# Bilinear operands written once and read with a repeating step, and matmul operands widened to 128 rows

## The chip, the cores and the metric

The kernel runs on one core of one Trainium2 chip. The metric is device time in microseconds of that core, from launch to end. A profile shows one execution of the same program: the busy times of the engines, the packets of the DMA queues, and what ended each engine's idle times. Engines are named as in the profile: PE is TensorE's matmul, PEld its load of the stationary operand, DVE is VectorE, ACT is ScalarE, POOL is GpSimd, SP is SyncE, which here only issues DMAs.

## The reference

The input is an image batch of shape (16, 56, 56, 128) in fp32. Four layers follow one another, each as `x = x + layer(group_norm(x))`:

- layer 0 is attention within shifted windows of 7 x 7 with 4 heads;
- layer 1 is a triangle update: a layer norm over the 128 channels, gated projections, a product over one image axis, a second layer norm, an output projection and a gate;
- layer 2 is a Fourier operator with an attention over the 56 rows and two spectral convolutions;
- layer 3 is the bilinear layer, which the change mostly concerns. Cut to what matters:

```python
xp = silu(x @ W1) @ W2
q, k, v = xp[..., :128], xp[..., 128:144], xp[..., 144:]   # each l2-normed; q is 8 heads of 16
K_H1 = conv2d(k, H1_w, groups=16) + P1                     # 3 x 7, per position a 16 x 16 matrix
kernel = einsum('xnk,xkd->xnd', q, K_H1)                   # per position x
feature = conv2d(v, H2_w)                                  # 16 x 16 per position
V_G = conv2d(v, G_w) + I                                   # 16 x 16 per position
feature = einsum('xvw,xvd->xwd', V_G, feature)
out = einsum('xnd,xvd->xvn', kernel, feature)
```

So each of the 3,136 positions of an image has three small products of an operand `y` with a matrix that a convolution of 21 taps (3 x 7) has made for that position.

## The kernel before, in words

An image lies in SBUF with the 128 channels on the partitions and its 3,136 positions along the free dimension, and is worked on in 7 chunks of 448 positions (`CH`, `NCH`). Images go through the four layers in turn. Each image belongs to one of two lanes (`lane[0] = b % 2`). A lane has its own arena of SBUF, its own five `w2` tiles of [128, 512], two PSUM banks `psb`, one PSUM tile `psd` of two banks, and twelve DRAM tiles `dy`. So two images are under way at a time. The order of the instructions on each engine isn't written out by hand: a planner runs through the program with its own estimates of the durations, gives out the tiles' buffers, and writes each engine's instructions in the order in which they came up there. On the chip each engine and each issuing queue (SP's, ACT's, POOL's) then keeps that order. The only orders given by hand are those of `together`, which lets the other matmuls of a group follow its first.

**The bilinear layer** (`_bilinear`). In the loop over `q`, chunk `q + 2` is projected (`project`), chunk `q - 2` goes through the feature product, chunk `q` through the kernel product, and chunk `q - 4` is finished (`last`).

`project` makes the 128 query rows of a chunk and hands them to `kept` (L1314 on): ACT copies them from PSUM to a `w2` tile `t` (L1317) and issues a DMA from ACT's queue (L1318) which writes the tile to DRAM eight times over: each row of `dy` is [8, 448], eight copies of one row of `t`. `project` also makes the 32 rows of k and v. PE turns them (L1361) to partitions 96 to 127 of a PSUM bank, ACT copies them (L1363) into one of two `staged` pieces of the arena, which sit in partitions 96 to 127 of its first 992 columns and have zeros at the borders, and three DMAs of ACT's queue (L1368) write them to the padded planes in DRAM.

`spread` (L1377) reads those planes back with four DMAs of SP's queue, so that each of 84 partitions of `im` holds one channel of k or v shifted by one of the 21 taps; row 84 holds ones and carries `P1` or `I`. The ones come from a memset of partitions 64 to 95 of the arena (L1304). `conv` multiplies these 85 rows by the weights `l3wk`, `l3wf` or `l3wg`: for `l3wf` two matmuls of 85 x 128 per half (L1391), otherwise groups of four of 85 x 32 through `together` (L368 the first, L371 the rest). ACT copies the result to `zs` (L1398).

`contract` forms one product. Four times it reads two of the four parts of `y` from DRAM into a buffer `rep` of [128, 2, 448] (L1410, SP's queue, four buffers), in which partition `a * 8 + k` holds row `a` of a part, for k from 0 to 7; DVE multiplies it by both halves of `z` (L1413, 128 x 1,792 elements, three buffers `prods`), and groups of eight matmuls by `red` (L368, L371) add up over the partitions into `acc`. The result of the first two products goes to DRAM through `kept` again.

**The layer norms** (`layer_norm` in `_triangle`, two per image). A matmul by `cen` takes off the mean; squares are averaged by matmuls that leave chunk `q` in row `32 * (q % 4) + q // 4` of one PSUM bank; ACT and DVE make 1/sqrt of it in `rs` (all 128 rows hold finite numbers). Then per chunk a matmul (L651) copies that one row of `rs` to all 128 partitions: its stationary operand is a column of the identity, stepped by 0 to 128 columns, of the 32 rows that hold it, and its moving operand the same 32 rows of `rs`. DVE multiplies (L652) and ACT scales (L653).

Of the kernel before, what the change touches and what calls it, by code (L numbers as in the profile page):

```python
# [36 lines left out]
F32 = mybir.dt.float32  # L37
# [5 lines left out]
P = 128  # L43
T = 56
# [3 lines left out]
CH = 448  # L48
# [156 lines left out]
def _weights(i):  # L205

    g = {k: np.asarray(v) for k, v in i.items()}
    w, early = {}, {}
# [20 lines left out]
    for n, key in (("a", "L2_conv_wQ"), ("b", "L2_conv_wK")):  # L229
        k = g[key][:, 0]  # L230
# [46 lines left out]

    wk3, wg3 = (np.zeros((85, 4, 2, 4, 8), np.float32) for _ in range(2))  # L280
    wf3 = np.zeros((85, 4, 16, 8), np.float32)
    for u in range(16):
        rows = slice(u % 4 * 21, u % 4 * 21 + 21)
        wk3[rows, u // 4, :, u % 4] = h1[u].reshape(2, 8, 21).transpose(2, 0, 1)
# [2 lines left out]
    wk3[84] = g["L3_conv_P1"][0].reshape(4, 4, 2, 8).transpose(0, 2, 1, 3)  # L287
    wg3[84] = g["L3_conv_I"][0].reshape(4, 4, 2, 8).transpose(0, 2, 1, 3)
    for n, v in (("l3wk", wk3), ("l3wf", wf3), ("l3wg", wg3)):
        w[n] = v.reshape(85, -1)  # L290
    return w, early, late


# [14 lines left out]
def tile_blocks(ctx: ExitStack, tc: tile.TileContext, ins, out, at, stages=(0, 1, 2, 3)):  # L308
# [22 lines left out]
    def uid(s):  # L331
        count[0] += 1
        return f"{s}{count[0]}"
# [14 lines left out]
        return ps2[lane[0]].tile([P, 2, 512], F32, tag="ps2", name=uid("psd"))  # L348

    def dram():  # L350
        return dyp[lane[0]].tile([P, 8 * CH], F32, tag="dy", name=uid("dy"))

    def bc(ap, axis, n):

# [260 lines left out]
def _triangle(env):  # L615
# [5 lines left out]
    def layer_norm(chunk, dst, sqs, lw, lb):  # L621


        for q in range(NCH):
            d, sq = dst[:, q * CH : (q + 1) * CH], sqs[:, q * CH : (q + 1) * CH]
            src = chunk(q)
            p = e.psb()
            mm(p[:, :CH], lhsT=C("cen"), rhs=src, start=True, stop=True)
            act(sq, p[:, :CH], AF.Square)
            nc.vector.tensor_copy(d, p[:, :CH])  # L630

        pv = e.psb()
        e.together(
            dict(
                out=pv[32 * (q % 4) : 32 * (q % 4) + 32, :CH],
                lhsT=C("oh")[:, 1 - q // 4 : 33 - q // 4],
                rhs=sqs[:, q * CH : (q + 1) * CH],
                start=q < 4,
                stop=q > 2,
            )  # L640
            for q in range(NCH)
        )
        rs = e.w2()
        act(rs[:, :CH], pv[:, :CH], AF.Sqrt, bias=eps)
        nc.vector.reciprocal(rs[:, :CH], rs[:, :CH])
        for q in range(NCH):
            d = dst[:, q * CH : (q + 1) * CH]
            s = slice(32 * (q % 4), 32 * (q % 4) + 32)
            p = e.psb()
            row = 32 * (q % 4) + q // 4  # L650
            mm(p[:, :CH], lhsT=C("ident")[s, row : row + 1].to_broadcast([32, P]), rhs=rs[s, :CH], start=True, stop=True)  # L651
            tt(d, d, p[:, :CH], ALU.mult)  # L652
            act(d, d, AF.Identity, bias=W("ln")[:, lb : lb + 1], scale=W("ln")[:, lw : lw + 1])  # L653

# [622 lines left out]
def _bilinear(env):  # L1277
# [20 lines left out]
    def run(b, xt):  # L1298
# [2 lines left out]
        kv_dram = padded[e.lane[0]]  # L1301

        im = [ar[:, 4 * SPAN * k : 4 * SPAN * (k + 1)] for k in range(2)]
        nc.gpsimd.memset(ar[64:96, 0 : 8 * SPAN], 1.0)  # L1304

        staged = [ar[96:P, k * SPAN : (k + 1) * SPAN] for k in range(2)]
        nc.gpsimd.memset(ar[96:P, 0 : 2 * SPAN], 0.0)
        zs = [ar[:, 3968 + k * 896 : 4864 + k * 896] for k in range(4)]
        reps = [ar[:, 7552 + k * 896 : 8448 + k * 896] for k in range(4)]
        prods = [ar[:, 11136 + k * 1792 : 12928 + k * 1792] for k in range(3)]  # L1310
# [3 lines left out]
        def kept(p):  # L1314

            t, d = e.w2(), e.dram()
            nc.scalar.copy(t[:, :CH], p[:, :CH])  # L1317
            nc.scalar.dma_start(out=d.rearrange("p (k t) -> p k t", k=8), in_=bc(t[:, :CH], 1, 8))  # L1318
            return d

        def project(q):
# [37 lines left out]
            p = e.psb()  # L1359
            for a in range(4):  # L1360
                mm(p[96:P, a * TT : (a + 1) * TT], lhsT=kv[:, a * 32 : (a + 1) * 32], rhs=C("ident")[:TT, :TT], start=True, stop=True)  # L1361
            t = staged[q % 2]
            nc.scalar.copy(  # L1363
                t.rearrange("p (r j) -> p r j", j=PITCH)[:, :, 3 : 3 + T],
                p[96:P, :CH].rearrange("p (r j) -> p r j", j=T),
# [16 lines left out]
        def conv(w, i, slot):  # L1382

            z = zs[slot]
            rows = im[i][:85].rearrange("p (g r j) -> p g r j", g=4, j=PITCH)[:, :, :, :T]
            wt = W(w)
            p = e.psd()
            for h in range(2):
                if w == "l3wf":
                    for g in (2 * h, 2 * h + 1):  # L1390
                        mm(p[:, h, :CH], lhsT=wt[:, g * P : (g + 1) * P], rhs=rows[:, g], start=g == 2 * h, stop=g == 2 * h + 1)  # L1391
                else:
                    e.together(
                        dict(out=p[32 * g : 32 * g + 32, h, :CH], lhsT=wt[:, (2 * g + h) * 32 : (2 * g + h + 1) * 32], rhs=rows[:, g], start=True, stop=True)
                        for g in range(4)
                    )
            z = z.rearrange("p (h t) -> p h t", h=2)
            nc.scalar.copy(z, p[:, :, :CH])  # L1398
            return z

        def contract(y, z):

            acc = e.psb()
            yv = y.rearrange("(i n a) (k t) -> n (a k) i t", n=2, a=D, k=8)
            for n in range(2):
                done = []
                for two in (0, 2):
                    rep = reps[count[1] % 4].rearrange("p (i t) -> p i t", i=2)
                    count[1] += 1
                    nc.sync.dma_start(out=rep, in_=yv[n][:, two : two + 2, :])  # L1410
                    t4 = prods[count[2] % 3].rearrange("p (i h t) -> p i h t", i=2, h=2)
                    count[2] += 1
                    tt(t4, bc(rep, 2, 2), bc(z, 1, 2), ALU.mult)  # L1413
                    done += [t4[:, 0], t4[:, 1]]
# [83 lines left out]
```

## Time and profile before

| what | value |
|---|---|
| median of 3 runs | 13,561.23 us (13,510.66 to 13,577.86) |
| the profiled execution | 13,592.43 us; span 13,590.7 us |
| PE busy | 10,774.2 us (79%), 82,624 matmuls |
| DVE busy | 9,629.1 us (71%) |
| ACT busy | 3,845.5 us (28%) |
| POOL busy | 1,391.0 us (10%) |
| mean granted TensorE clock | 0.832 |
| DMA | 1,091,753 packets, 2,105.90 MB |
| of it dy written (ACT's queue, q10) | 336 DMAs of 1,792 KB |
| of it dy read (SP's queue, q1) | 1,344 DMAs of 448 KB |
| of it padded planes read (q1) | 896 DMAs of 162.8 KB |
| of it Fourier table (POOL's queue, q0) | 2,048 DMAs of 294 KB |

The page cuts the span into 40 equal slices of 340 us; each digit is a tenth of busy time in a slice, or of the full clock. A pair of images takes some 1,700 us, five slices. A line of a group gives the line of the code, engine, operation, result and operands with their shapes, how often, then the busy time, the mean duration in ns, and the engine's idle time just before with what ended it. q1 is SP's DMA queue, q10 ACT's, q0 POOL's; a line of a queue gives packets, MB and the share of the time of all 16 DMA engines.

### The profile page before, as it was taken

The page shows a single profiled execution, that of the slowest core. Times are in us where ns is not written, and L with a number is a line of the kernel's source. Part 1 is how long each engine was busy: PE and PEld are TensorE (multiplying, and loading weights), DVE is VectorE, ACT ScalarE, POOL GpSimd, SP SyncE. Part 2 cuts the span into 40 slices and gives each one's busy share as a digit, 9 for nine tenths or more (in the row PEclk, how much of TensorE's full clock was granted, in tenths as well). Part 3 has the DMA queues.
Part 4 walks back from the last instruction along what each step waited for, and adds up shares of the span by engine and source line. Part 5 has one row for each costly group of instructions (what it writes and reads, how often), then busy time and mean ns, then how long its engine had stood idle before and what let it go on. Part 6 is the DMA issues. An engine that isn't in the chain of part 4 may idle for free. (4 is left out here: it accounts for less than half of the span.)

```text
span 13590.7 us, 201886 instructions
## 1 busy us (share of the span) xinstructions
PE 10774.2 (79%) x82624; PEld 5938.7 (44%) x82624; DVE 9629.1 (71%) x13985; ACT 3845.5 (28%) x6630; POOL 1391.0 (10%) x2650
## 2 busy tenths in 40 slices
PE   7888787886878878887788877887777887778876
PEld 4454254542545335443354433544335543355432
DVE  7776868757686685776767768667686676866766
ACT  4232141321423223232242322322224222242221
POOL 0120002200022000220002200022000220002200
PEclk9887888878988887887888888878788888888877
DMA  1246804378044770447704577044680446804468
GB/s 34 85 149 243 294 1 125 115 252 278 5 130 111 265 261 5 118 132 250 267 7 117 143 270 237 7 117 128 222 293 13 117 128 230 288 10 117 132 230 276
DMA packets 1091753, 2105.90 MB, mean 155 GB/s; under 512 B 98320, under 2 KB 974096, under 8 KB 1089680
## 3 DMA queue, kind: packets, MB, share of 16 engines
q1 hardware_dynamic: 560000, 823.95, 18.5%
q0 software_dynamic: 165120, 629.61, 17.1%
q10 hardware_dynamic: 365712, 639.44, 13.0%
q8 instruction: 654, 10.72, 0.3%
q14 instruction: 267, 2.19, 0.1%
HBM read 1412.73 MB, written 667.03 MB: 153 GB/s over the span
## 5 line engine op out<-in xcount | busy, mean ns | idle before, releaser
L1413 DVE TENSOR_TENSOR arena<-arena 128x1792 f32<-128x1792 f32 x1344 | 2656.5, 2018 | 713.8 <-PE psb L371 314.6
L1203 DVE TENSOR_TENSOR arena<-arena 112x1344 f32<-112x1344 f32 x1024 | 1571.3, 1553 | 383.1 <-DMA arena<-table 372.6
L371 PE MATMUL psb<-arena,cst 128*32 128x448 f32 x9792 | 1600.8, 682 | 0.0
L368 PE MATMUL psb<-arena,cst 128*32 128x448 f32 x1408 | 836.6, 683 | 766.2 <-DVE arena L1413 675.2
L1201 POOL DMA_DIRECT2D arena<-table x2048 | 1064.8, 521 | 2647.2 <-PE psb L1117 610.6
L371 PE MATMUL psb<-arena 112*64 112x224 f32 (+2 forms) x4864 | 1252.8, 528 | 0.0
L368 PE MATMUL psb<-arena 112*64 112x448 f32 (+1 forms) x1280 | 697.5, 630 | 368.7 <-DVE arena L1094 178.5
L371 PE MATMUL psd<-arena 112*64 112x224 f32 (+1 forms) x3072 | 746.7, 464 | 0.0
L368 PE MATMUL psd<-arena 112*64 112x448 f32 x1024 | 552.4, 625 | 214.3 <-DVE arena L1203 200.9
L371 PEld LDWEIGHTS psb<-arena 112*64 112x64 f32 (+1 forms) x4864 | 440.9, 153 | 512.8 <-issue 509.7
L1094 DVE TENSOR_TENSOR arena<-w,coef 128x1792 f32<-128x1792 f32 x256 | 507.6, 2020 | 190.9 <-PE psb L371 167.4
L679 PE MATMUL psd<-wgt,arena 128*64 128x128 f32 x7168 | 549.8, 303 | 102.9 <-DVE arena L691 79.4
L368 PEld LDWEIGHTS psb<-arena,cst 128*32 128x32 f32 x1408 | 123.3, 122 | 1137.4 <-DVE arena L1413 818.2
L1398 ACT COPY arena<-psd 128x896 f32<-128x896 f32 x336 | 303.5, 906 | 1022.2 <-DVE arena L1413 581.4
L371 PEld LDWEIGHTS psb<-arena,cst 128*32 128x32 f32 x9792 | 373.6, 127 | 485.9 <-issue 468.5
L679 PEld LDWEIGHTS psd<-wgt,arena 128*64 128x64 f32 x7168 | 472.0, 151 | 246.1 <-issue 163.8
L371 PE MATMUL psd<-arena,wgt 85*32 85x448 f32 x2688 | 528.6, 624 | 40.7 <-DMA arena<-padded 40.1
L908 PE MATMUL psb<-cst,arena 128*128 128x64 f32 (+1 forms) x2688 | 452.9, 341 | 55.5 <-ACT arena L918 30.6
L908 PEld LDWEIGHTS psb<-cst,arena 128*128 128x128 f32 x2688 | 438.7, 255 | 104.6 <-issue 51.7
L368 PE MATMUL psd<-arena,wgt 85*32 85x448 f32 x896 | 449.8, 619 | 41.6 <-DMA arena<-padded 34.1
L1317 ACT COPY w<-psb 128x448 f32<-128x448 f32 x336 | 178.7, 532 | 1032.5 <-PE psb L371 728.8
L589 PE MATMUL psb<-cst,arena 128*49 128x128 f32 x2048 | 345.5, 326 | 146.1 <-DVE arena L584 87.7
(299 smaller groups left out, 19630.8 us busy)
## 6 DMA issues: line engine op xcount, KB each, us to landing
arena<-table POOLq DMA_DIRECT2D x2048, 294.0 KB, 9.1
dy<-w ACTq DMA_DIRECT2D x336, 1792.0 KB
arena<-dy SPq DMA_DIRECT2D x1344, 448.0 KB
arena<-padded SPq DMA_DIRECT2D x896, 162.8 KB
w<-x SPq DMA_DIRECT2D x112, 224.0 KB
out<-w SPq DMA_DIRECT2D x112, 224.0 KB
padded<-arena ACTq DMA_DIRECT2D x336, 62.0 KB
arena<-arena POOLq DMA_DIRECT2D x16, 784.0 KB, 9.9
```

The lines of the kernel that those rows point to most:

```text
L368: done = mm(**first)
L371: mm(**kw)
L589: nc.tensor.transpose(p[:WIN, i * P : (i + 1) * P], s3[:, 4 * g + i, :], C("ident"))
L679: mm(p[half : half + 64, i // 4, i % 4 * P : (i % 4 + 1) * P], lhsT=xh[:, c0 : c0 + 64], rhs=W(w).rearrange("p (k c) -> p k c", c=64)[:, : ...
L908: mm(p[:, 2 * i * nl : 2 * (i + 1) * nl], lhsT=src[:, t * P : (t + 1) * P], rhs=fc, start=True, stop=True)
L1094: tt(t4, bc(ys[c][:, l0 : l0 + 4, :], 1, 8), bc(coef[:, c, h0 : h0 + 8, l0 : l0 + 4], 3, T), ALU.mult,)
L1201: nc.gpsimd.dma_start(out=t[hh * T : (hh + 1) * T, :], in_=bc(tflat[q, two, hh], 0, T))
L1203: tt(t4, bc(x3[:, :, s], 1, 2), t4, ALU.mult)
L1317: nc.scalar.copy(t[:, :CH], p[:, :CH])
L1398: nc.scalar.copy(z, p[:, :, :CH])
L1413: tt(t4, bc(rep, 2, 2), bc(z, 1, 2), ALU.mult)
```

## The change

Four edits, in the words of the code:

- `dy` becomes [128, 448] instead of [128, 3,584]. `kept` writes each row once. Row p of `t` is i * 32 + r, with i the part (0 to 3); it now goes to place (r, i), so that the four parts of one row lie side by side. `contract` reads two parts at once as 896 elements in a row, and names each row eight times by a step of 0 in the source.
- The weights `l3wk`, `l3wf`, `l3wg` get 128 rows, of which rows 85 to 127 are zero, and `conv` multiplies all 128 rows of `im`. So the memset of ones covers partitions 64 to 127, and rows 85 to 127 hold ones against weights of zero.
- With partitions 96 to 127 of the arena taken by these ones, the staging tile of k and v becomes a `w2` tile of each chunk, zeroed by a memset on POOL before ACT's copy.
- The norms' spread takes all 128 rows of the identity's column and of `rs` in place of 32.

```diff
-    wk3, wg3 = (np.zeros((85, 4, 2, 4, 8), np.float32) for _ in range(2))
-    wf3 = np.zeros((85, 4, 16, 8), np.float32)
+    wk3, wg3 = (np.zeros((P, 4, 2, 4, 8), np.float32) for _ in range(2))
+    wf3 = np.zeros((P, 4, 16, 8), np.float32)
...
-        w[n] = v.reshape(85, -1)
+        w[n] = v.reshape(P, -1)
...
-        return dyp[lane[0]].tile([P, 8 * CH], F32, tag="dy", name=uid("dy"))
+        return dyp[lane[0]].tile([P, CH], F32, tag="dy", name=uid("dy"))
...
-            s = slice(32 * (q % 4), 32 * (q % 4) + 32)
             p = e.psb()
             row = 32 * (q % 4) + q // 4
-            mm(p[:, :CH], lhsT=C("ident")[s, row : row + 1].to_broadcast([32, P]), rhs=rs[s, :CH], start=True, stop=True)
+            mm(p[:, :CH], lhsT=C("ident")[:, row : row + 1].to_broadcast([P, P]), rhs=rs[:, :CH], start=True, stop=True)
...
-        nc.gpsimd.memset(ar[64:96, 0 : 8 * SPAN], 1.0)
-
-        staged = [ar[96:P, k * SPAN : (k + 1) * SPAN] for k in range(2)]
-        nc.gpsimd.memset(ar[96:P, 0 : 2 * SPAN], 0.0)
+        nc.gpsimd.memset(ar[64:P, 0 : 8 * SPAN], 1.0)
...
-            nc.scalar.dma_start(out=d.rearrange("p (k t) -> p k t", k=8), in_=bc(t[:, :CH], 1, 8))
+            nc.scalar.dma_start(out=planes(d, 0, ((CH, 4), (4 * CH, 32), (1, CH))), in_=t[:, :CH])
...
-            t = staged[q % 2]
+
+            t = e.w2()[96:P, :SPAN]
+            nc.gpsimd.memset(t, 0.0)
...
-            rows = im[i][:85].rearrange("p (g r j) -> p g r j", g=4, j=PITCH)[:, :, :, :T]
+            rows = im[i].rearrange("p (g r j) -> p g r j", g=4, j=PITCH)[:, :, :, :T]
...
-            yv = y.rearrange("(i n a) (k t) -> n (a k) i t", n=2, a=D, k=8)
...
-                    rep = reps[count[1] % 4].rearrange("p (i t) -> p i t", i=2)
+                    rep = reps[count[1] % 4]
                     count[1] += 1
-                    nc.sync.dma_start(out=rep, in_=yv[n][:, two : two + 2, :])
+                    nc.sync.dma_start(out=rep, in_=planes(y, (n * D * 4 + two) * CH, ((4 * CH, D), (0, 8), (1, 2 * CH))))
+                    rep = rep.rearrange("p (i t) -> p i t", i=2)
```

## The prediction

> **What bounds the kernel now.** I read the page's slices first, then its queues, then the bilinear stage of one pair of images in stretches of 100 us, then the waits, and last the chain of the final pair. The slices (DVE, granted clock, DMA share) repeat every five: the two last of each five are the bilinear stage.
>
> ```profile
> DVE  7776868757686685776767768667686676866766
> PEclk9887888878988887887888888878788888888877
> DMA  1246804378044770447704577044680446804468
> q1 hardware_dynamic: 560000, 823.95, 18.5%
> q0 software_dynamic: 165120, 629.61, 17.1%
> q10 hardware_dynamic: 365712, 639.44, 13.0%
> ```
>
> No engine is full on average, but DMA stands at 7 to 8 tenths in the bilinear slices, and inside them (columns: window, PE, PEld, DVE, ACT, POOL busy, clock, DMA share, GB/s) it fills up:
>
> ```profile
> 4500.00:4600.00 100.00, 79.83 (x378) 39.52 (x378) 58.30 (x110) 20.50 (x37) 4.32 (x2) 0.77 0.78 271
> 4700.00:4800.00 100.00, 81.07 (x496) 33.15 (x492) 67.22 (x63) 16.63 (x26) 0.00 (x0) 0.83 0.95 325
> 4800.00:4900.00 100.00, 68.92 (x472) 24.89 (x464) 84.18 (x62) 15.42 (x25) 0.00 (x0) 0.85 1.00 357
> ```
>
> DVE does 58 to 84 us of 100, PE 69 to 81, DMA 78 to 100: three near-limits, of which DMA is the only one that reaches its end. Who waits for it, over the whole span (busy, mean ns, idle before):
>
> ```profile
> L1413 DVE TENSOR_TENSOR arena<-arena 128x1792 f32<-128x1792 f32 x1344 | 2656.5, 2018 | 713.8 <-PE psb L371 314.6 <-DMA arena<-dy 264.5 <-ACT arena L1398 110.0
> L371 PE MATMUL psd<-arena,wgt 85*32 85x448 f32 x2688 | 528.6, 624 | 40.7 <-DMA arena<-padded 40.1
> L368 PE MATMUL psd<-arena,wgt 85*32 85x448 f32 x896 | 449.8, 619 | 41.6 <-DMA arena<-padded 34.1 <-ACT arena L1398 7.4
> L651 PE MATMUL psb<-w,cst 32*128 32x448 f32 x448 | 219.2, 804 | 76.2 <-DVE w L645 51.1 <-DVE arena L652 18.3 <-DVE sm L1053 4.4
> L990 PE MATMUL psb<-arena,cst 128*128 128x448 f32 x672 | 367.6, 672 | 39.2 <-DVE arena L987 13.7 <-ACT arena L985 12.2 <-ACT arena L1022 6.9
> ```
>
> The page's chain sums to a fifth of the span only, the last stretch, so I read it for the last two pairs' bilinear windows of 720 us. In the last, `DMA arena<-dy` holds 10.8%, `DMA dy<-w` 8.7% and `DMA arena<-padded` 4.2%: 78, 63 and 30 us; in the pair before 76, 24 and 24. Average: 77 + 44 + 27 = 148 us a pair. Single writes of dy held it for 7 to 18 us.
>
> **The Trainium skill.** (1) TensorE: Matmul & The Clock Gate, Part 1 (The HAM clock gate): an activity monitor gives the array half or full clock, by windows of 3,413 ns. The trace agrees: its clock record knows only 0.5 and 1.0, in steps of 3.413 us, 34% of them at half, and a 448-column matmul took 539 ns at full and 954 at half. (2) The same page, Part 3 (Packing small matmuls): [...]several run at once. It agrees: 301 of L651's 448 matmuls overlap the next (219.2 us covered, 448 x 804 ns = 360 in sum). (3) DMA: Bandwidth & Descriptors, Why a DMA increments its semaphore by 16: a transfer uses the largest k up to 16 that divides both sides' slowest dimension. It agrees: q10's 365,712 packets are 336 x (1,024 + 16) for dy, 336 x (32 + 16) for the planes, 144 for the weights, so one packet of semaphore for each of 16 engines.
>
> **The change part by part.**
>
> Writes of dy. Now 336 x 1,024 = 344,064 packets at q10's mean (13.0% x 16 x 13,590.7 us / 365,712) = 77 ns: 1,656 us of all 16 engines, 207 a pair. After: 128 packets each, 207 us in all. The new destination's slowest dimension is 4, so by (3) only four engines carry it: 32 packets, 2.5 us, where 64 on each of 16 took 4.9. Those four get 103 us a pair, less than the 207 before. DMA saved: 1,449 us, 181 a pair.
>
> Reads of dy. Bytes stay (616.6 MB), packets go from 256 of 1,792 B to 128 of 3,584 B; 16 engines still (16 divides 128). Whether eight reads of one place cost more, no dy row shows; the nearest is the Fourier table, whose rows are read 56 times. q1 takes 2,514 us for 824 MB, 3.05 us/MB; the table 3.69. So 1,881 us before, between 10% less (fewer packets) and 2,276 (+395) after. I take +100; DMA net -1,350.
>
> What that moves: the chain. A write falls from 12.5 us (the mean of seven) to about 5 (2.5 plus the 1.7 us in which the small padded writes land on the same chain, and some queueing), 44 to 18 us a pair; reads, queued less, from 7.0 to 4.5, 77 to 50; padded from 27 to 20. That is 60 us a pair, 480 in all, if nothing else takes over. It will: PE is 69 to 81% busy there, and L1413 also waits 314.6 us for PE and 110 for ACT. The direct waits (264.5 + 40.1 + 34.1 = 339 us) are the other measure; 60% of them is 203. I take 300.
>
> Staging through w2. One 0.92 us memset per image goes; the 3.40 us one covers 64 rows for 32 at the same length; seven memsets of [32, 496] come, 0.46 us each (half of 992 columns at 920 ns). They lie between the squares (L1345) and the copy (L1363), 1.6 to 20 us, median 8.7 apart, so 0 on the path. Without that cover: 112 x 0.46 = 52 us. If one is late, L1363 is, and behind it on ACT the padded writes and the other image's copies; DVE and PE wait for those. A staged tile holds one of five w2 slots until its writes land; a dy tile holds its own for fewer us. Even.
>
> Issue. L1318 blocks ACT's queue 0.52 us, L1410 SP's 0.365; three-dimensional L1377 takes 0.76. At worst +0.25 x 336 = 84 us on ACT (28% busy) and +0.4 x 1,344 = 538 on SP, 34 an image of some 550: no cost, unless padded reads (on SP behind them) get late, +20.
>
> Convolutions at 128 rows. Same columns, same time at a clock. What can move is the gate. I summed per 3.413 us step, over the matmul records, active rows x columns / 16,384 x 1.25 ns a moving column. This ranks a warm next step above a cold one in 98% of cases from warm (94% from cold); with rows ignored 97% (87%). The state flips near 0.43 to 0.50 of the array. With 128 rows in both edits, the same curve leaves 384 us fewer at half clock (143 from the convolutions, 241 from the norms) of 4,540. Each such us of matmuls shrinks to 0.56; PE holds 9 of the chain's 21 parts: 384 x 0.44 x 0.43 = -70. If rows don't count: 0.
>
> Norms' spread. 448 matmuls that overlapped take turns now: at the present half-and-half clock 448 x 745 ns = 334 us for 219, warm 260. On its own image it stays under ACT's L653 (755 ns); the other image's PE work is delayed by a third of 40 to 115 us: +20 (0 to 115).
>
> Sum: -300 - 70 + 20 = -350. Against the profiled execution's span of 13,590.7 (1.7 us lie around it): 13,241. The runs' median is 0.23% below that execution: 13,210.
>
> **Rivals.** *Hidden* (0.15): the planner's order and PE set the stage; PE is near 80% busy at a clock of 0.77 where DVE has only 58, and the saved DMA waits return as waits for PE. Gain 30 to 100: about 13,500. *POOL's queue* (0.15), slower: POOL's order is written by the planner, and a staging memset may stand behind the other image's arena memset or L536, which wait up to 107.7 us (L1304 for PE) and 56 us (81 waits, 1,328.6 us). From 26 us per image (418/16) the change ends slower by 0.5%; 35 us give 13,770. Against it: POOL is otherwise idle there, and memsets are planned by readiness. A reordered plan in general goes here. *Repeated reads* (0.10), slower: above 310 ns per 3,584 B packet ((207 + 235 - 26) us x 16 / 21,504) DMA is as full as before; the table's rate means 211, today's 175. Then about 13,750. *The forecast* (0.60): 12,950 to 13,450.
>
> **How the numbers follow.** Within 0.5% is what a measurement can't tell from no change (13,493 to 13,629). Faster: 0.60 + 0.06 of hidden = 0.66; same: 0.09 of hidden and 0.01; slower 0.24. The range runs from 12,950 to 13,700, leaving out some 0.05 below and 0.12 above; the forecast's own is 12,950 to 13,450.
>
> **What would show it.** q10 at about 60,600 packets (336 x (128 + 4) for dy if four engines carry it) and 100 MB; q1 at 388,000; total near 1,566 MB; DMA slices at 4 to 6; L1413's wait for dy under 100 us; clock from 0.832 to about 0.86; L651 at 128 rows, 540 to 700 ns; L1363 with no wait for POOL. Wrong if L1413's idle time keeps its 714 us under other names, if ACT waits for POOL, or if the packets of the reads pass 210 ns.

## The result, and the profile after

| | before | after |
|---|---|---|
| median, 14 runs each | 13,577.55 us (13,510.66 to 13,612.31) | 13,655.42 us (13,602.10 to 13,721.09) |
| profiled span | 13,590.7 us | 13,715.4 us |
| mean granted TensorE clock | 0.832 | 0.835 |

The changed kernel takes 1.0059 times as long (95% interval 1.0039 to 1.0079): some 80 us slower, where 350 us less were forecast. The profiled execution of after is one of its longer ones; the two spans differ by 125 us, the medians by 78.

The page of the changed kernel, its slices and queues:

```profile
DVE  7866867777666776767767676676766767767675
PEclk9987888888887888977888788897788878888877
DMA  1354704455045550455504455045550445504545
q1 hardware_dynamic: 387968, 823.95, 21.1%
q0 software_dynamic: 165120, 629.61, 17.2%
q10 hardware_dynamic: 60624, 99.93, 2.6%
```

The transfers did what the change says. ACT's queue (q10) writes 100 MB where it wrote 639, and the bilinear slices stand at 4 to 5 tenths of DMA (after the first pair) where they stood at 6 to 8. The same three stretches of a pair's bilinear stage (columns: window, PE, PEld, DVE, ACT, POOL busy, clock, DMA share, GB/s):

```profile
4500.00:4600.00 100.00, 80.31 (x695) 46.08 (x693) 60.13 (x99) 29.36 (x54) 2.00 (x5) 0.82 0.49 139
4700.00:4800.00 100.00, 72.41 (x436) 30.15 (x429) 68.24 (x77) 16.90 (x30) 1.52 (x3) 0.83 0.66 195
4800.00:4900.00 100.00, 72.76 (x428) 37.59 (x427) 59.80 (x105) 24.15 (x41) 4.83 (x11) 0.76 0.43 119
```

DMA has room now, 0.43 to 0.66, and yet PE and DVE aren't busier than before: averaged over the three stretches PE does 75 us of 100 where it did 77, DVE 63 where it did 70 (the lanes stand differently, so a stretch doesn't hold quite the same work in both). The groups that wait (busy, mean ns, idle before, and what ended it):

```profile
L1411 DVE TENSOR_TENSOR arena<-arena 128x1792 f32<-128x1792 f32 x1344 | 2665.3, 2019 | 942.9 <-PE psb L371 400.8 <-DMA arena<-dy 299.6 <-ACT arena L1396 212.2
L371 PE MATMUL psd<-arena,wgt 128*32 128x448 f32 x2688 | 508.1, 615 | 39.7 <-DMA arena<-padded 39.4
L368 PE MATMUL psd<-arena,wgt 128*32 128x448 f32 x896 | 448.1, 617 | 92.4 <-DMA arena<-padded 89.9 <-ACT arena L1396 2.3
L650 PE MATMUL psb<-w,cst 128*128 128x448 f32 x448 | 208.7, 577 | 34.9 <-DVE w L645 32.0 <-DVE arena L651 2.9
L989 PE MATMUL psb<-arena,cst 128*128 128x448 f32 x672 | 356.0, 659 | 78.5 <-ACT arena L984 33.2 <-ACT arena L1021 22.1 <-DVE arena L1245 11.3
```

The products of the bilinear stage (L1413 before, L1411 now) wait 943 us where they waited 714: for dy 300 us instead of 265, although dy's transfers are lighter, for PE 401 instead of 315, for ACT 212 instead of 110. PE's waits for padded keys (L371 and L368 with `psd`) went from 74 us to 129. No single new wait has taken the place of an old one; most of the old ones have grown.

One more view tells what kind of thing has changed. Each image's bilinear stage begins with POOL's memset of ones, so its start times mark where the two lanes stand. Its line for the last pair, images 14 and 15, before (durations in ns, then first and last start in us):

```profile
L1304 POOL MEMSET arena<- x2: 3398/3398/3398, 12839.4 to 13128.1; 32x3968 f32 x2
```

and after:

```profile
L1303 POOL MEMSET arena<- x2: 3404/3404/3404, 12876.5 to 13303.4; 64x3968 f32 x2
```

The odd lane stands 289 us behind the even one before, 427 us after. Nothing in the four edits moves a lane against the other. The order of the instructions does: the planner, given other instructions, has written another one.

### The profile page after: what moved, and what is told of

Same layout as the page of the kernel before. It is cut to its first block, busy times and chain, and to the rows that moved or that the text cites. A ratio compares the mean times of both kernels' runs of the same rounds, so it can differ in the third digit from the quotient of the medians.

```text
span 13715.4 us, 202688 instructions
## 1 busy us (share of the span) xinstructions
PE 10697.2 (78%) x82624; PEld 5921.2 (43%) x82624; DVE 9630.0 (70%) x13985; ACT 3916.2 (29%) x6686; POOL 1460.0 (11%) x2746
## 3 DMA queue, kind: packets, MB, share of 16 engines
q10 hardware_dynamic: 60624, 99.93, 2.6%
## 5 line engine op out<-in xcount | busy, mean ns | idle before, releaser
L1411 DVE TENSOR_TENSOR arena<-arena 128x1792 f32<-128x1792 f32 x1344 | 2665.3, 2019 | 942.9 <-PE psb L371 400.8
L371 PE MATMUL psb<-arena,cst 128*32 128x448 f32 x9792 | 1626.3, 688 | 0.0
L368 PE MATMUL psb<-arena,cst 128*32 128x448 f32 x1408 | 840.5, 686 | 828.2 <-DVE arena L1411 723.1
L371 PE MATMUL psb<-arena 112*64 112x224 f32 (+2 forms) x4864 | 1291.3, 537 | 0.0
L368 PE MATMUL psb<-arena 112*64 112x448 f32 (+1 forms) x1280 | 721.9, 651 | 425.4 <-DVE arena L1093 214.5
L371 PE MATMUL psd<-arena 112*64 112x224 f32 (+1 forms) x3072 | 773.1, 476 | 0.0
L368 PE MATMUL psd<-arena 112*64 112x448 f32 x1024 | 568.4, 641 | 204.0 <-DVE arena L1202 192.6
L371 PEld LDWEIGHTS psb<-arena 112*64 112x64 f32 (+1 forms) x4864 | 448.3, 156 | 526.3 <-issue 520.6
L368 PEld LDWEIGHTS psb<-arena,cst 128*32 128x32 f32 x1408 | 119.9, 121 | 1180.1 <-DVE arena L1411 891.0
L678 PE MATMUL psd<-wgt,arena 128*64 128x128 f32 x7168 | 509.4, 290 | 107.4 <-DVE arena L690 100.6
L371 PEld LDWEIGHTS psb<-arena,cst 128*32 128x32 f32 x9792 | 377.1, 127 | 486.7 <-issue 469.2
L371 PE MATMUL psd<-arena,wgt 128*32 128x448 f32 x2688 | 508.1, 615 | 39.7 <-DMA arena<-padded 39.4
L368 PE MATMUL psd<-arena,wgt 128*32 128x448 f32 x896 | 448.1, 617 | 92.4 <-DMA arena<-padded 89.9
```

The source lines that it names most:

```text
L368: done = mm(**first)
L371: mm(**kw)
L678: mm(p[half : half + 64, i // 4, i % 4 * P : (i % 4 + 1) * P], lhsT=xh[:, c0 : c0 + 64], rhs=W(w).rearrange("p (k c) -> p k c", c=64)[:, : ...
```

## The experiments

All ratios are to the kernel before, run on the same chip in the same batch; its median lies between 13,560 and 13,578 us in every batch, so ratios of different batches can be compared. Where spans or waits are compared, they are those of one profiled execution of each kernel; that of after is 60 us above its median. The diffs are abridged: `NoSync` and `only` stand for longer expressions. All kernels do the whole work of the reference. Those of the experiments have a few lines more than the two kernels, so L1432 or L1444 in their profiles are the products (L1413 before), and L374 and L371 the members and the first of `together`.

### The edits, or the order they were put in

The planner's order was taken apart from the edits. A kernel is planned, each engine's order is kept as a list of instruction numbers, and another kernel with the same instructions in number is planned with that list as a constraint. The constraint adds an edge from each instruction to the next on its engine, without any semaphore:

```diff
+    for e, ks in order.items():
+        for a, b in zip(ks, ks[1:]):
+            tc.add_manual_dep(mine[e][b], mine[e][a].name, NoSync, reason="order")
```

Only the staging memsets, which one kernel has in other numbers than the other, are left to the planner. The traces show that the order was taken over: compared place by place by operation, tiles and shape, VectorE's 13,985 instructions and SP's 2,506 in e1 come in the sequence of the kernel before, and those of e2 in that of the changed kernel; the changed kernel itself has only 2,330 of VectorE's at the place where the kernel before has them. e1 is the changed kernel in the order of the kernel before, e2 the kernel before in the order of the changed one. e3 has the bilinear operands alone (the edits of `dram`, `kept` and `contract`), e4 the convolutions alone (the weights, `conv`, the memsets, the staging), each in the order that the planner makes for it.

> All four edits, but every engine and queue keeps the order that the planner wrote for the kernel before (order-only edges; only the 112 new staging memsets on POOL are placed freely). Theory plan (the edits are a gain of about 50 us of each image's bilinear layer, and the changed kernel lost it because the planner wrote another order): ratio to before 0.97 to 0.985, about 13,250 us. Theory edits (the repeated reads at 199 ns a packet and the staging cost what the writes gain, the order is beside the point): 1.000 to 1.010, about 13,650 us.

> The kernel before, instruction for instruction, in the order that the planner wrote for the changed kernel. Theory plan: slower than both, ratio 1.015 to 1.04, 13,800 to 14,100 us, since the worse order is there and the saved transfers are not. Theory edits: 0.995 to 1.005.

> Only the first edit: dy written once, read with the repeating step; convolutions at 85 rows, staging in the arena, the norms' spread at 32 rows; the planner's own order for it. Theory plan: this edit changes the planner's estimates most, so the order moves as in the changed kernel: 1.000 to 1.010. Theory edits, reads to blame: 1.003 to 1.010 as well; staging to blame: 0.97 to 0.985.

> Only the convolutions at 128 rows and with them the staging tile in w2; dy written eight times, the norms' spread at 32 rows; the planner's own order. Theory plan: within 0.99 to 1.01, as the order falls. Theory edits, staging to blame: 1.010 to 1.03, with ACT's copy of the staged rows waiting. If the clock follows the declared rows, mean clock above 0.838.

| work, order | ratio (95% interval) |
|---|---|
| e1: changed, before's order | 0.9823 (0.9786 to 0.9861) |
| e2: before's, changed order | 1.0222 (1.0189 to 1.0256) |
| e3: bilinear operands, own order | 1.0198 (1.0164 to 1.0233) |
| e4: convolutions, own order | 1.0004 (0.9984 to 1.0024) |

e3 was slower than either theory had it. e4 lies where "plan" had it, but its granted clock (median 0.8315) did not pass the 0.838 that was expected if the clock follows the rows. The answers of e1 and e2 are clear. In the old order the edits gain 1.8% (240 us of 13,571). With no edit at all, the new order costs 2.2%. Their product is 1.004; the changed kernel has 1.006. The groups of e1:

```profile
L1432 DVE TENSOR_TENSOR arena<-arena 128x1792 f32<-128x1792 f32 x1344 | 2654.8, 2019 | 557.5 <-PE psb L374 303.9 <-DMA arena<-dy 147.9 <-ACT arena L1412 87.3
L374 PE MATMUL psd<-arena,wgt 128*32 128x448 f32 x2688 | 486.1, 591 | 22.9 <-DMA arena<-padded 22.3
L371 PE MATMUL psd<-arena,wgt 128*32 128x448 f32 x896 | 426.5, 592 | 42.2 <-DMA arena<-padded 34.1 <-ACT arena L1412 8.1
```

With the same instructions as the changed kernel, the products wait 558 us, not 943, and for dy 148, not 300. In e2 the instructions are those of the kernel before, and the wait for dy grows from 265 to 416:

```profile
L1432 DVE TENSOR_TENSOR arena<-arena 128x1792 f32<-128x1792 f32 x1344 | 2670.5, 2021 | 1057.7 <-DMA arena<-dy 416.0 <-PE psb L374 403.8 <-ACT arena L1412 212.9
```

So e1 is faster than both kernels, by edits that are the change's own.

### What each edit gains in the old order

Three kernels with one group of edits each, in the order of the kernel before.

> The bilinear operands written once with repeating reads alone, without the convolutions and norms, in the order of the kernel before. It splits the 1.8% that the whole change gains in that order. 'The gain is the transfers' (shorter write, a read that doesn't wait): 0.980 to 0.988, nearly all of it, with VectorE's waits for dy down by some 100 us. 'The gain is the clock' (convolutions at 128 rows keep TensorE's clock up): 0.997 to 1.002 here, and the rest in the run of the convolutions.

> The convolutions over 128 rows (with the weights' zero rows, the ones below them and the staging in a work tile) alone, without the bilinear operands and norms, in the order of the kernel before. 'The gain is the clock': 0.984 to 0.990, granted clock 0.845 or more. 'The gain is the transfers': 0.996 to 1.002, granted clock 0.83 to 0.84. My estimate on record for the clock part was 70 us, 0.995.

> The layer norms' spread over 128 rows alone, in the order of the kernel before. The whole change gains 1.77% there; the bilinear operands alone gained 0.79% and the convolutions 0.45%, which leaves 0.5%. 'The parts add up': 0.993 to 0.997, with a higher clock. My estimate on record was a loss of 20 us (0 to 115): 1.0015, at most 1.0085. 'The parts help each other' (the rest comes only when dy and the clock go together): 0.998 to 1.002.

| edit alone, before's order | ratio (95% interval) | us | median clock of its runs |
|---|---|---|---|
| none | 1 | | 0.831 |
| e7: bilinear operands | 0.9921 (0.9891 to 0.9951) | -107 | 0.835 |
| e8: convolutions, with the staging | 0.9955 (0.9937 to 0.9973) | -61 | 0.838 |
| e11: norms' spread | 0.9961 (0.9942 to 0.9981) | -53 | 0.839 |
| sum | 0.984 | -221 | |
| e1: all | 0.9823 (0.9786 to 0.9861) | -240 | 0.851 |

The parts add up, as e11's first expectation had it. Neither pure theory of e7 and e8 holds: about half of the gain comes with the transfers and half with the wider matmuls. In e7 the wait for dy falls by 131 us (265 to 133.5):

```profile
L1444 DVE TENSOR_TENSOR arena<-arena 128x1792 f32<-128x1792 f32 x1344 | 2653.7, 2018 | 589.9 <-PE psb L374 328.5 <-DMA arena<-dy 133.5 <-ACT arena L1424 111.0
```

In e8 the products' idle time hardly changes (714 to 683 us), and the matmuls of the convolutions get shorter, 624 to 609 ns. In the records of before and e8 a matmul of 448 columns takes 538 or 539 ns at full clock and 954 at half (medians), with 85 rows as with 128, so what has changed is how much of it runs at full clock:

```profile
L374 PE MATMUL psd<-arena,wgt 128*32 128x448 f32 x2688 | 509.7, 609 | 28.1 <-DMA arena<-padded 27.9
```

In e11 the estimate on record, a loss of 20 us, was a miss. The spread at 128 rows is busy 235 us, only 16 more than the 219 at 32 rows, and each matmul takes 640 ns where it took 804:

```profile
L663 PE MATMUL psb<-w,cst 128*128 128x448 f32 x448 | 235.2, 640 | 70.7 <-DVE w L657 52.0 <-DVE arena L664 11.9 <-DVE sm L1065 4.4
```

Since e3 and e7, and e4 and e8, are the same work in two orders, the order that the planner makes for the bilinear operands alone costs 2.8% (1.0198 / 0.9921), and the one for the convolutions 0.5%.

### The distance of the lanes

The distance was the first suspect. Two kernels change it, with one edge added and the planner free otherwise: the first `bn_stats` of one image's stage is kept behind the 61st product of the image before.

```diff
             i = nc.vector.bn_stats(out=st[:, q * 6 : q * 6 + 6], in_=xt[:, q * CH : (q + 1) * CH])
+            if hold is not None and q == 0:
+                tc.add_manual_dep(i.ins, hold.name, NoSync, reason="hold")
```

e5 is the changed kernel with the even lane held at its window attention, so that the distance stays small; e6 is the kernel before with the odd lane held at its bilinear stage, so that it grows. e12 is the kernel before in the order that the planner makes for the norms' edit, a new order that has nothing to do with the transfers.

> All of the change, in the order that the planner chooses for it, with one constraint: on VectorE the first statistics instruction of an even image's window attention is kept behind the 61st of the 84 products of the odd image's contraction before it. The planner's own order for the changed kernel puts only 43, 11, 7, 0, 0, 0, 0 of those products ahead (images 2, 4 to 14), for the kernel before 65, 63, 55, 31, 31, 23, 23; with the constraint it is 61 for each. Theory 'distance of the lanes' (the changed kernel's order is bad because the two images that are worked on at once stand too far apart, so that one's contraction falls on the other's contraction and its window attention gets no partner): the time comes down to that of the changed work in the kernel before's order, 0.980 to 0.990 of before. Rival 'order in detail' (the loss sits in how single instructions are interleaved, in many places, and the distance is only a by-product): the constraint mends little, 1.000 to 1.015.

> The kernel before, none of the change, planned anew with one constraint that makes the distance what it is in the changed kernel: the first statistics instruction of an odd image's bilinear stage is kept behind the 61st product of the even image's contraction. The planner then puts 3, 0, 3, 0, 0, 3, 0 of the odd image's products ahead of the next even image's window attention, as in the changed kernel's order (43, 11, 7, 0, 0, 0, 0). 'Distance of the lanes': 1.015 to 1.03, as the kernel before in the whole of the changed kernel's order (1.022). 'Order in detail': the planner has only this one constraint to meet and fits everything else around it: 0.995 to 1.010.

> The kernel before, none of the change, in the order that the planner makes for another small edit (the norms' spread alone). Its distance of the lanes is between the two kernels' (63, 31, 31, 19, 19, 19, 3), and 47% of VectorE's neighbouring pairs are as in the kernel before. It measures what a new plan costs that was not made for these transfers. 'A new plan is a draw': between 0.995 and 1.02, most likely 1.005 to 1.012 (the kernel before is among the better draws). 'The changed kernel's order is bad for a reason of its own' (the planner's prices for the new transfers): 0.997 to 1.003.

e5 took 0.9985 (0.9967 to 1.0003), e6 1.0092 (1.0057 to 1.0128), e12 1.0082 (1.0056 to 1.0108). e12 is where "a draw" expected it. The constraint did to the distance what it was meant to do. The memset of the last pair in e5:

```profile
L1320 POOL MEMSET arena<- x2: 3404/3404/3404, 12838.1 to 13089.3; 64x3968 f32 x2
```

and in e6:

```profile
L1322 POOL MEMSET arena<- x2: 3397/3397/3397, 12884.7 to 13273.4; 32x3968 f32 x2
```

It is 251 us in e5 (427 without the hold) and 389 in e6 (289 without). The time followed in both directions, but by less than "distance" expected: e5 mends 0.7% of 2.4%, e6 loses 0.9% where the whole order loses 2.2%. e6 still lies within what "detail" expected, e5 between the two. So the distance is a part of the effect, a third or somewhat more. Where it acts can be read by adding up a span from the same starts: the even lane's first bilinear start, the seven steps from there to its last one, the distance to the odd lane's last one, and the rest.

| us | first | seven pairs of the even lane | distance in the last pair | rest | span |
|---|---|---|---|---|---|
| before | 1,048 | 11,791 | 289 | 463 | 13,591 |
| after | 1,058 | 11,818 | 427 | 412 | 13,715 |
| e1: changed, old order | 1,058 | 11,565 | 282 | 438 | 13,343 |
| e2: old, changed order | 1,045 | 11,967 | 438 | 426 | 13,876 |
| e5: changed, held | 1,043 | 11,795 | 251 | 460 | 13,549 |
| e6: old, pushed | 1,070 | 11,815 | 389 | 419 | 13,692 |
| e3: bilinear operands, own order | 1,053 | 11,816 | 607 | 375 | 13,851 |
| e7: bilinear operands, old order | 1,053 | 11,695 | 290 | 438 | 13,476 |
| e12: old, norms' order | 1,056 | 11,776 | 431 | 402 | 13,666 |

The pace of the even lane hardly follows the distance: e5 against after and e6 against before differ by only 23 and 24 us over seven pairs (their plans differ in other waits too, so this is a net). It costs once, at the end, where the odd lane finishes alone: 176 us less distance and 48 more of rest in e5, 100 more and 44 less in e6. e12's whole loss is of this kind (142 more, 61 less, and no slower pace), and in e3, where the odd lane ends up 607 us behind, it is 254 of the 375 us that it loses to e7. The changed kernel against e1 is 373 us longer: 145 - 26 = 119 at the end, and 253 by a slower pace of the even lane. The pace was still without a cause. A lower granted clock (medians 0.8365 in after, 0.8505 in e1) is not enough as a cause: e5 has 0.850, and its seven pairs take 230 us longer than e1's.

### One queue's or one engine's order alone

Two kernels with the changed work took over the old order only in part: e9 on SP's and POOL's queues, e10 on VectorE.

```diff
     for e, ks in order.items():
+        if e not in only:
+            continue
```

> All of the change; the order of the kernel before is imposed on the transfers alone (SP's queue and POOL's, and POOL's few instructions), and the planner is free on VectorE, ScalarE and TensorE. The lanes' distance that it then plans is that of the kernel before (65, 63, 55, 31, 29, 19, 19 of the odd image's products ahead of the next even image's window attention), while of the neighbouring pairs of instructions of the kernel before's VectorE order only 62% stay neighbours (45% in the changed kernel). Theory 'the queues' (what is left after the distance is when dy's reads are asked for): 0.980 to 0.988 of before, with VectorE's idle time put to dy near 150 us. Rival 'the engines' (what is left is how VectorE's and ScalarE's instructions of the two images are interleaved): 0.990 to 1.000, with dy's share at 250 us or more. 'Distance alone' would be 0.998, as the run with the hold.

> All of the change; the order of the kernel before is imposed on VectorE's instructions alone, and the planner is free elsewhere; of SP's neighbouring pairs 76% stay as in the kernel before (66% in the changed kernel), of ScalarE's 88%. 'The engines': 0.980 to 0.986, all of what the full order gives. 'The queues': 0.988 to 0.998.

e9 took 1.0098 (1.0073 to 1.0123), e10 1.0013 (0.9989 to 1.0037), with distances near the old one (331 and 295 us in the last pair). Both theories missed both times: with either half of the old order the kernel is 1.9 to 2.8% slower than with all of it. In e9 the products waited 656 us for dy. In e10 they waited 648 us in all, not much more than e1's 558, but TensorE waited 257 us for padded keys where it waited 56 in e1. The products of e9, and the first matmuls of the convolutions in e10:

```profile
L1444 DVE TENSOR_TENSOR arena<-arena 128x1792 f32<-128x1792 f32 x1344 | 2663.1, 2019 | 1109.1 <-DMA arena<-dy 655.9 <-PE psb L374 329.6 <-ACT arena L1424 113.0
L371 PE MATMUL psd<-arena,wgt 128*32 128x448 f32 x896 | 459.4, 630 | 205.2 <-DMA arena<-padded 204.3 <-ACT arena L1424 0.9
```

I take from this that not the order of one engine counts, but that SP's queue and the engines fit each other. That is argued, not shown.

### Two places in SP's queue

SP's queue is in order, and holds the reads of dy and the reads of padded keys of both lanes. How often it stood at a read of keys that had not been written yet differs between the orders (us in total, times, longest). Before:

```profile
SPq L1377 <- DMA padded<-arena: 879.2, 58, 37.0
```

After:

```profile
SPq L1375 <- DMA padded<-w: 1595.9, 111, 40.7
```

e1 has 54 such waits, e2 114. So it looked as if the standing queue delayed dy. Three kernels keep an order on every engine, and move only the four reads of keys of a convolution behind the next two reads of dy; three others move them ahead of the last two. A later place is never behind a read that itself waits for that convolution. Order and work are the changed kernel's (e13, e16), the changed kernel's with the hold (e14, e17), and the changed work in the old order (e15, e18).

```diff
+    group = [f, f + 1, f + 2, f + 3]
+    out[at:] = rest[:passed] + group + rest[passed:]
```

is the move to a later place, `f` being the first of the four reads and `passed` the place behind the second read of dy; to an earlier one it is

```diff
+    out = head[:cut] + group + head[cut:] + tail
```

> All of the change in the changed kernel's own order on every engine, but on SP's queue the four reads of the padded keys for a convolution are put behind the next two reads of dy (206 of 224 such groups can be moved). Theory 'the standing queue' (SP stands at a read whose keys are not yet written, 111 times and 1,596 us in the changed kernel, and dy's reads behind it come late): the waits fall to fewer than 60, VectorE's idle time put to dy from 300 to 200 us, the time from 1.006 to between 0.993 and 1.000. Rival 'late keys' (what stands at the head was the most urgent read; behind two others it comes later still): TensorE's waits for padded keys grow from 130 us to over 250, the time is 1.006 to 1.02.

> The same move in the plan with the lanes' distance held (which took 0.9985). 'The standing queue', with the distance as the only other part: 0.984 to 0.992. 'Late keys': 0.998 to 1.012.

> The same move in the order of the kernel before (0.982 for the changed work). SP stood there 54 times, 874 us. 'The standing queue': a small gain, 0.975 to 0.982. 'Late keys': 0.983 to 0.995.

> All of the change in the changed kernel's own order, with the four reads of the padded keys put before the two reads of dy that stood ahead of them in SP's queue (197 of 224 groups can be moved). Theory 'keys too late' (TensorE's 129 us of waits for keys, against 56 in the old order, are paid in full): the waits fall to 60 to 90 us and the time by as much, from 1.006 to 1.001 to 1.003. Rival 'the reads stood there anyway' (what is late is the writing of the keys; an earlier read only stands longer and holds up dy): waits for keys as before, those for dy up from 300 to 400 us or more, 1.008 to 1.020.

> The same move in the plan with the distance held (0.9985, waits for keys 167 us). 'Keys too late': 0.990 to 0.995. 'The reads stood there anyway': 1.000 to 1.012.

> The same move in the order of the kernel before (0.982, waits for keys 56 us). 'Keys too late': 0.979 to 0.983. 'The reads stood there anyway': 0.985 to 0.995.

| keys moved | ratio (95% interval) | span, against the unmoved order | TensorE's wait for keys | products' wait for dy |
|---|---|---|---|---|
| e13: changed order, later | 1.0231 (1.0216 to 1.0246) | +179 us | 129 to 357 us | 300 to 275 us |
| e14: held, later | 1.0186 (1.0154 to 1.0218) | +300 | 167 to 425 | 397 to 325 |
| e15: old order, later | 0.9924 (0.9894 to 0.9953) | +160 | 56 to 207 | 148 to 100 |
| e16: changed order, earlier | 1.0359 (1.0304 to 1.0415) | +424 | 129 to 110 | 300 to 798 |
| e17: held, earlier | 1.0259 (1.0221 to 1.0297) | +315 | 167 to 139 | 397 to 817 |
| e18: old order, earlier | 1.0034 (1.0013 to 1.0054) | +242 | 56 to 52 | 148 to 539 |

The first theory, that standing costs by itself, fell with e13: SP stood 13 times instead of 111, and the kernel was 1.7% slower than the changed one. The lines of e13:

```profile
L1444 DVE TENSOR_TENSOR arena<-arena 128x1792 f32<-128x1792 f32 x1344 | 2660.8, 2018 | 1046.8 <-PE psb L374 462.3 <-DMA arena<-dy 274.9 <-ACT arena L1424 244.0
L371 PE MATMUL psd<-arena,wgt 128*32 128x448 f32 x896 | 486.8, 661 | 343.4 <-DMA arena<-padded 343.4
```

and the queue's waits in the same run:

```profile
SPq L1402 <- DMA padded<-w: 316.2, 13, 43.1
```

"Late keys" was right, in e13 and e14 by more than it expected, in e15 within its range: the keys came later, and TensorE paid for it. In e16 it is the other way round, as "the reads stood there anyway" had it:

```profile
L1444 DVE TENSOR_TENSOR arena<-arena 128x1792 f32<-128x1792 f32 x1344 | 2664.7, 2019 | 1412.5 <-DMA arena<-dy 797.9 <-PE psb L374 407.0 <-ACT arena L1424 184.1
L371 PE MATMUL psd<-arena,wgt 128*32 128x448 f32 x896 | 457.8, 630 | 68.1 <-DMA arena<-padded 67.7 <-ACT arena L1424 0.3
```

TensorE's wait for keys falls by only 19 us: SP stands at their reads for longer, as they are not written yet:

```profile
SPq L1402 <- DMA padded<-w: 1857.6, 114, 34.9
```

The products' wait for dy grows by 498 us. "Keys too late" predicted a gain and fell in all three runs, and the losses are larger than the rival had them. Both moves lose in all three orders. But the six runs give the prices of the two waits. Moving later added 636 us of waits for keys in the three runs (228, 258, 150), took 145 off dy, and cost 639 us of span: 1 us or more for each us of keys. Moving earlier added 1,309 us of waits for dy (498, 420, 391), took 51 off keys, and cost 980: some 0.75 us for each.

With these prices a part of the pace can be accounted for. Against e1 the changed kernel has 73 us more of waits for keys and 152 more for dy: 73 + 0.75 x 152 = 187 of the 253 us. e2 against before: 41 + 0.75 x 151 = 154 of 176. The others fit badly: e10 against e1 gives 200 + 29 = 229 for 144 us of pace, e5 110 + 187 = 297 for 230, e9 139 + 381 = 520 for 280. A third wait is left out here, that of the Fourier layer's products for their table. In the changed kernel:

```profile
L1202 DVE TENSOR_TENSOR arena<-arena 112x1344 f32<-112x1344 f32 x1024 | 1573.4, 1553 | 465.8 <-DMA arena<-table 452.5 <-PE psb L371 5.0 <-DVE w L1222 1.5
```

and in e1:

```profile
L1206 DVE TENSOR_TENSOR arena<-arena 112x1344 f32<-112x1344 f32 x1024 | 1571.7, 1554 | 393.9 <-DMA arena<-table 382.9 <-PE psb L374 3.2 <-PE psd L374 2.5
```

It is 373 us before, 403 in e2, 342 in e5, 285 in e10 and 380 in e9. At 1 us for each us, a price that no run here measures, the sums become 257 of 253, 185 of 176, 131 for 144 and 256 for 230; e9 stays at 517 for 280. So this is an account, found after the runs, and not a measurement of each part: that these waits carry most of the lost pace is argued, and e9 speaks against the prices. Why the planner's new order lets them grow stays open: its own estimates of the transfers are not in any profile.

## Why the prediction was wrong

**The step that failed is the one ahead of all others: the sum was made on the order of the kernel before.** "What that moves: the chain" and every later term take each instruction's neighbours from the trace of before. The planner gave the changed kernel another order, for which the sum has no term, and this cost 2.4% (1.0059 / 0.9823), some 320 us, more than all edits gain (240). Of these about a third is the lanes' distance at the end, and the rest a slower pace, for which the longer waits for dy, padded keys and the table are an account and not a proof. The prediction has it only as a clause in a rival at 0.15, "A reordered plan in general goes here", and priced there a POOL memset in place of it. e1 and e2 show it in both directions. In the old order the change (13,319 us) lies inside the forecast's range, but in part by luck, since its terms miss in opposite directions. Point by point, the terms against the runs in the old order, which is the one they were made for:

- *Bound*: DMA was full in its stretches (shares of 0.78 to 1.00), but making room there was worth only 0.8% (e7).
- *Writes of dy*: right. q10's share times the span was 13.0% of 13,590.7 = 1,767 us and is 2.6% of 13,715.4 = 357: 1,410 saved, 1,449 forecast. The 60,624 packets are 336 x (128 + 4) for dy, 336 x (32 + 16) for the planes and 144 for the weights, so four engines carry each write, as the Trainium skill has it ("DMA: Bandwidth & Descriptors", Why a DMA increments its semaphore by 16): the largest k up to 16 that divides the slowest dimension, here 4.
- *Reads of dy*: direction right, size wrong. q1 went from 2,514 to 2,894 us, +380, where +100 was taken for dy's reads and +395 was the upper end. In the packet records dy's reads are 317 of it: a packet of 3,584 B takes 199 ns on average, where two of 1,792 B took 85 each. So DMA saved 1,030 us net, not 1,350.
- *The chain*: right mechanism, three times too large. Taken were 300 us, between 480 by the chain and 203 by the direct waits. e7 shows 107 (66 to 148). The wait for dy fell by 131 us of 265, and the waits for padded keys hardly fell (74 to 71), though the chain had them at 27 us a pair and the forecast took 7 off. Read as in the forecast, the chain of e7's last two pairs holds 68 us a pair for reads of dy, 27 for writes and 29 for padded reads (windows 12,755 to 13,475 and 11,072 to 11,792 us): 25 less than before, not 60. The writes fell by 17 of the 26 forecast, the reads by 9 of 27: the reads are what was mis-sized most. The waits were the better measure, and even of these only 134 of 339 us went.
- *Staging, issue*: even, as forecast. e8 contains the staging and is faster. A memset takes 506 ns (0.46 us forecast) and waits long for its `w2` slot (2,360 us in all for earlier writes of dy), but of ACT's copy no wait is put to it (8.6 us are put to other work of POOL). The read's issue takes 515 ns where it took 365, within the forecast's bound, and e7, which has it, is faster.
- *Convolutions at 128 rows, norms' spread*: right mechanism, too small. Together -70 + 20 = -50 were forecast; e8 and e11 show -61 and -53. The spread was to keep PE busy for 260 to 334 us, and does for 235 in e11 (at the 539 ns of full clock 448 matmuls are 241 us, not 260); its net of +20 and its share of the clock's gain was near -24 (241 of 384 us at half clock), and -53 was measured. The clock rose to 0.838 and 0.839 for the two edits alone and to 0.851 for all; 0.86 was forecast.
- *Sum*: -350 forecast, -240 in the old order (190 to 290). The chain's term was 193 us too large, the terms at 128 rows 64 too small.
- *Rivals*: "Hidden" is partly true: half of dy's waits stayed, though the products' waits for PE grew by only 14 us in e7. "Repeated reads" did not decide: 199 ns is far below its 310. "POOL's queue" did not come true as a mechanism, as said under staging; what came true is the clause that was put with it.
- *What would show it*: q10, q1, the total of 1,566 MB, DMA slices at 4 to 5 and L650 at 577 ns came as said. The wait for dy below 100 us (300) and the clock of 0.86 (0.835) did not. The sign named for a wrong forecast was there: the products' idle time kept its 714 us, and grew to 943.

## What to carry to other kernels

When a planner writes the order, an edit is two changes: the work and a new order, and the second can be the larger one (here -1.8% and +2.4%). The order of the kernel before was one of the better ones: for the same work each of the four orders that the planner made for other edits is slower than it, by 0.5% (e4), 0.8% (e12), 2.4% (after) and 2.8% (e3). Measure the edit with the old order imposed before judging it, and if it gains there, keep that order: e1 is the same change at 0.982. In this in-order queue, which feeds two consumers, two places either way cost 1 to 3%, so a queue that stands at its head is no proof that its head should be moved.

## What the runs showed that was not expected

- Rows that add nothing to the result go with a higher granted clock. In e8 43 of 128 rows multiply ones by zeros, and the median clock goes from 0.831 (0.825 to 0.836 over 88 runs of before in two batches) to 0.838 (0.836 to 0.844 over 20); the norms' spread, with 127 such rows where it had 31, gives 0.839 (0.831 to 0.842 over 16). In the changed order it is 0.8205 without the edits (e2) and 0.8365 with them (after). An order moves it as well: e4 has e8's edits and 0.8315. The Trainium skill's page "TensorE: Matmul & The Clock Gate", The HAM clock gate, speaks of activity; that a row of zeros counts as active is what e8 and e11 suggest, though e8 has the new staging too and in e11 the spread's matmuls overlap less.
- The spread at 128 rows keeps PE hardly busier than the one at 32 rows, whose matmuls overlap more: 235 us against 219, since a matmul took 640 ns in place of 804. 448 x 640 ns are 287 us, so even at 128 rows neighbours overlap in the record.
- Reading one place eight times costs 17% at most here: 199 ns for a packet of 3,584 B, against 170 for the two packets that carried the same bytes without repetition. Not all of it need be the repetition: the padded reads' packets of 1,984 B, which the change leaves alone, went from 95 to 105 ns.
- The reads of keys and of dy share one queue so closely that two places cost 160 to 300 us one way and 240 to 420 the other. The largest loss expected in the changed order was 1.4% in both directions; it was 1.7% and 3.0%.
